# Last MLP of a four-layer network: its norm moved beside the products of the MLP in front of it, a second PSUM bank, its load and stores on another queue

## The chip, the core and the metric

The kernel runs on one core of a Trainium2 chip. The metric is the device time of one execution in microseconds. A core has engines that run side by side[...]: PE (matrix products into PSUM), DVE (VectorE), ACT (ScalarE), POOL (GpSimd) and SP, which here only issues transfers. Transfers are issued from SP, ACT and POOL and carried by 16 DMA engines. [...]a bank that a product was summed in has to be read out by ACT or DVE before the next product may use it.

## What is computed

The reference is a chain of four layers on x of shape 8 x 384 x 32 x 32, all in float32. Layers 0 and 1 are state-space ("Mamba") blocks over 1024 tokens per image; layer 1 ends in a norm and an MLP. Layers 2 and 3 are depthwise convolutions, with a 1x1 convolution between them. What bears on the change is the end of layer 1 and the start of layer 2:

```python
# layer 1, per image, tokens xs of width 384
mo = mo * (1.0 + mod[:, None, :])          # output products of the Mamba block, gated
xs = xs + mo
h = _ln(xs, n3_g, n3_b)
h = jax.nn.gelu(h @ fc1_w.T + fc1_b) @ fc2_w.T + fc2_b
xs = xs + h
# layer 2, on all 8 images
out = bn_eval(dwconv(x, w_lk, 1), ...)     # and six smaller depthwise kernels, summed
```

## The kernel before

Channels lie on the 128 partitions, so 384 channels are 3 blocks. Tokens are cut into halves of 512. A *unit* is one half image in one of the Mamba layers; there are 32, layer 0 and layer 1 interleaved. An *MLP* belongs to one half image of layer 1; there are 16. Each unit is a row of 48 items of its scan, and each item is a slot. All other work (norms, products, copies, loads, stores) is put into slots of this clock with `put(slot, function, ...)`, from a table `AT` of offsets; within a slot, entries marked `first` go ahead. The slots then fix the order of instructions on every engine; nothing is reordered later. When the units are over, the slots that are left are emitted in order: the output products of the last unit, the rest of the MLP in front of the last (first half of image 7) and the whole last MLP (second half of image 7).

The output products of a unit (`out_product`, line 599) are three blocks m of 6 products each in PSUM pool `mm` (two banks), with weights `wo`; each block also has a load of the residual (`residual`), on ACT a bias (`out_gate`), on DVE the sum (`out_add`) and on SP a store to `x2` (`out_store`). `AT['out']` gives the three blocks' slots: 0, 5 and 9.

An MLP has these steps. `norm` (line 726) issues the load of three blocks into tile `mx` (one buffer, so that it waits for the MLP in front), the mean (3 products), `centre` on DVE, three squares on ACT each followed by a variance product, then ACT's `rs_tables` and `rs_exp`, four operations `rs_newton` on POOL (line 396) and three `scale` on POOL (line 408). `mlp_up` (line 692) makes 12 products of 3 steps each with weights `wi` (five buffers); `mlp_raw` on ACT copies each out of its bank into `fh`; four batches of gelu on ACT work on three tiles each, with a table load before and after. `mlp_down` (line 705) makes 3 output blocks of 12 steps from `fh` and weights `wo` (six slices, three buffers). `mlp_out` on DVE adds bias and residual `mo` (one buffer) into the tile `rows_out` (one buffer), and `mlp_store` (line 719) sends it to `x3`, 16 rows of 38 floats in each partition. Products of all MLPs are summed in one bank, pool `m_f`:

```python
ps_f = st.enter_context(tc.tile_pool(name="m_f", bufs=1, space=PSUM))
```

All these loads and stores are on SP's queue, in the order of the slots.

The depthwise layers are a class of their own, `Depthwise`, whose instructions are emitted after all slots. On POOL it clears four image tiles `xp` (line 952), then `early` issues the weight windows `wt` of the first ten groups (line 959, four loads each), then three tiles `q_out` of the 1x1 convolution are cleared (line 1020), and then `images` (line 973) loads image rows from `x3`, two loads a group. A group is 8 channels, so 16 groups need only the first block of `x3`. Weights of later groups are loaded from SP and ACT, ten groups ahead. Per group DVE shifts copies (lines 988 to 990), PE makes 32 products (line 997), ACT copies them out and stores.

Of the kernel before, what the change touches and what calls it, by code (L numbers as in the profile page):

```python
# [9 lines left out]
F32 = mybir.dt.float32  # L10
AF = mybir.ActivationFunctionType
ALU = mybir.AluOpType
# [4 lines left out]
P = 128  # L17
B = 8
C = 384
# [6 lines left out]
T = 512  # L26
NU = B * L // T
# [39 lines left out]
class Plan:  # L67
# [6 lines left out]
    def put(self, slot, f, *args, first=False):  # L74
        self.slots.setdefault(slot, ([], []))[0 if first else 1].append(lambda: f(*args))
# [141 lines left out]

AT = {'in_ahead': 3, 'out_ahead': 2, 'taps_ahead': 4, 'norm': (-5, -2, -1, 0, 1, 2, 3, 3, 5, 5, 7, 7, 11, 12, 13), 'x': (14, 16, 18, 24, 26, 29), 'shift': 1, 'conv': 4, 'u': 5, 'silu': ((28, 3, 0), (34, 6, 0), (40, 6, 3), (57, 6, 6)), 'hid': 2, 'ranks': (33, 34, 35), 'z': (31, 34, 36, 38, 40, 41), 'B': (40, 43, 47, 48), 'C': (42, 45, 47, 52), 'repeat': (9, 12, 12, 13), 'out': (0, 5, 9), 'out_half': 3, 'out_add': 4, 'out_gate': 2, 'res_ahead': 1, 'heads': 15, 'softmax': (17, 18, 19), 'attend': (19, 22, 25, 26), 'context': 28, 'hidden': (29, 30, 32, 35, 36, 39), 'gates': (47, 41, 46), 'mlp': 22, 'mlp_norm': (-7, 0, 1, 2, 3, 4, 5, 5, 5, 6, 6, 10, 10, 12, 12), 'mlp_plan': ((3, 62, 12, (21, 31, 42, 69), -2), (2, 42, 6, (26, 30, 42, 46), -2), (2, 40, 4, (24, 26, 34, 40), -2), (2, 40, 3, (24, 26, 34, 36), -2), (2, 42, 7, (22, 28, 36, 36), -2)), 'fold0': (-145, -128), 'shifted': 1, 'bc_out': 37, 'store': 2, 'px_ahead': 2, 'pool': (0, 4), 'norm0': (-97, -89, -86, -85, -83, -80, -77, -75, -74, -73, -72, -71, -69, -69, -68), 'soft': ((37, 2), (45, 4), (62, 6)), 'du': 1, 'du_pace': 0, 'flat_u': 1, 'inject': 0, 'y': 25, 'fold': 0, 'var': 1, 'down_gap': 0, 'first': {'x': [2, 4, 7, 10, 13, 16], 'silu': [[14, 3, 0], [22, 6, 0], [34, 6, 2], [44, 6, 6]], 'ranks': [22, 24, 25], 'z': [29, 31, 31, 33, 34, 35], 'soft': [[29, 2], [33, 4], [60, 6]], 'bc_out': 29, 'B': [32, 34, 36, 39], 'repeat': [0, 0, 0, 1], 'C': [38, 43, 43, 46]}, 'fold0_step': (1, 7), 'norm1': (-3, -1, 0, 1, 2, 3, 4, 4, 8, 8, 10, 10, 12, 13, 13), 'prepare': (-40, 4),  # L220
}


def layers(tc, k, a, vec, x0, x1, x2, x3, lasting, got):
# [8 lines left out]
    nc = tc.nc  # L233
# [7 lines left out]
    with ExitStack() as st:  # L241
# [5 lines left out]
        ps_f = st.enter_context(tc.tile_pool(name="m_f", bufs=1, space=PSUM))  # L247
# [8 lines left out]
        t = tile("fh")  # L256
# [25 lines left out]
        rows_out = wp.tile([P, T // HW, WIDE], F32, name="rows_out")  # L282
# [15 lines left out]
        hid = wp.tile([P, KD], F32, name="hid")  # L298

        def mm():  # L300
            return ps_mm.tile([P, T], F32, tag="mm", name="mm")
# [62 lines left out]

        def load(s, src, tag):
            s.xt = work.tile([P, KC, T], F32, tag=tag, name=tag, bufs=1)
            nc.sync.dma_start(s.xt, src.rearrange("(c p) t -> p c t", p=P)[:, :, s.cols])

        def mean(s):
            s.mean = mm()  # L370
# [25 lines left out]
        def rs_newton(s, step):  # L396

            if step == 0:
                s.rt = work.tile([P, T], F32, tag="sq", name="sq", bufs=1)
                nc.gpsimd.tensor_tensor(s.rt, s.ry, s.ry, ALU.mult)  # L400
            elif step == 1:
                nc.gpsimd.tensor_tensor(s.rt, s.rt, s.rv, ALU.mult)
            elif step == 2:
                nc.gpsimd.tensor_scalar(s.rt, s.rt, -0.5, 1.5, ALU.mult, ALU.add)
            else:
                nc.gpsimd.tensor_tensor(s.ry, s.ry, s.rt, ALU.mult)

        def scale(s, c):
            nc.gpsimd.tensor_tensor(s.xt[:, c], s.xt[:, c], s.ry, ALU.mult)


        def product(s, m):
# [274 lines left out]
        class Mlp:  # L687
            def __init__(self, b, half):
                self.b, self.half, self.cols = b, half, slice(half * T, (half + 1) * T)
                self.w, self.ps, self.hs = {}, {}, [None] * KF  # L690

        def mlp_up(s, m, c):
            if c == 0:
                s.ps[m] = ps_f.tile([P, T], F32, tag="f", name="f")
            nc.tensor.matmul(s.ps[m], s.w["in", m][:, c], s.xt[:, c], start=c == 0, stop=c == KC - 1)  # L695

        def mlp_raw(s, m):
# [6 lines left out]

        def mlp_down(s, m, f):
            if f == 0:
                s.down = ps_f.tile([P, T], F32, tag="f", name="f")
            nc.tensor.matmul(  # L708
                s.down, s.w["out", 2 * m + f // KD][:, f % KD], s.hs[f], start=f == 0, stop=f == KF - 1
            )  # L710
# [7 lines left out]

        def mlp_store(s, m):
            n = T // HW  # L720
            nc.sync.dma_start(x3[m * P : (m + 1) * P, s.half * n : (s.half + 1) * n, s.b, :], rows_out)


        put = plan.put

        def norm(s, src, tag, at, slots):

            slots = iter([at + e for e in slots])
            put(next(slots), load, s, src, tag)
            put(next(slots), mean, s)  # L730
            put(next(slots), centre, s, first=True)
            for c in range(KC):
                e = next(slots)
                put(e, square, s, c)
                put(e + AT["var"], variance, s, c, first=AT["var"] > 0)
            put(next(slots), rs_tables, s, first=True)
            put(next(slots), rs_exp, s)
            for step in range(4):
                put(next(slots), rs_newton, s, step)
            for c in range(KC):  # L740
                put(next(slots), scale, s, c)
# [12 lines left out]
        for j, s in enumerate(folds):  # L754
            for m in range(2 * KD):
                at = (j - 1) * SLOTS + 7 + 2 * m if j else AT["fold0"][m // KD] + AT["fold0_step"][m // KD] * (m % KD)
# [9 lines left out]
        for b in range(1, B):  # L766
            order += [(1, b - 1), (0, b + 1)] if b < B - 1 else [(1, b - 1), (1, b)]
        units = [Unit(both[n], b, half) for n, b in order for half in range(L // T)]
        done = {(s.layer.gated, s.b, s.half): i for i, s in enumerate(units)}
        assert len(units) == 2 * NU  # L770

        for i, s in enumerate(units):

            lay, at = s.layer, (i - 1) * SLOTS
            first = AT if i else {**AT, **AT["first"]}
            norm(s, lay.src[s.b], "xt", at, AT["norm"] if i > 1 else AT[f"norm{i}"])
            for d in range(KD):
                e = at + first["x"][d]
# [44 lines left out]
            for d in range(KD):  # L823
                at = i * SLOTS + (d - 2) * PER
# [4 lines left out]
                put(at + AT["y"], y_out, s, d, first=True)  # L829

            at = (i + 1) * SLOTS
            for m in range(KC):
                e = at + AT["out"][m]
                put(e - AT["res_ahead"], residual, s, m)
                if lay.gated:
                    put(e + AT["out_gate"], out_gate, s, m)
                use_out(e, s, m, lay.w["out"][m])
                for j in range(2):
                    put(e + AT["out_half"] * j, out_product, s, m, j)
                put(e + AT["out_add"], out_add, s, m, first=True)  # L840
                put(e + AT["out_add"] + AT["store"], out_store, s, m, first=True)
            if not lay.gated:
                continue

# [28 lines left out]
        for b in range(B):  # L873
            for half in range(L // T):
                s = Mlp(b, half)
                at = max(at, (done[True, b, half] + 1) * SLOTS + AT["mlp"])
                if (at - AT["mlp"]) % SLOTS > 20:
                    at += (AT["mlp"] - at) % SLOTS
                pace_up, down, pace_down, tables, gap = AT["mlp_plan"][max(b - B + 4, 0) + (b == B - 1) * half]
                norm(s, x2[b], "mx", at, AT["mlp_norm"])  # L880
                for m in range(KF):
                    e = at + 12 + pace_up * m
                    use_in(e, s, m, fc1_w[m])
                    for c in range(KC):
                        put(e + c * pace_up // KC, mlp_up, s, m, c)
                    put(e + 2 * pace_up // KC + 1, mlp_raw, s, m, first=True)
                for j, e in enumerate(tables):
                    put(at + e, table, lambda s=s, j=j: s.hs[3 * j : 3 * j + 3], AF.Gelu_apprx_tanh)
                for m in range(KC):
                    e = at + down + (pace_down + AT["down_gap"]) * m  # L890
                    put(e, mlp_residual, s, m)
                    for f in range(KF):
                        if f % KD == 0:
                            use_out(e + f * pace_down // KF, s, 2 * m + f // KD, a["fc2"][2 * m + f // KD])
                        put(e + f * pace_down // KF, mlp_down, s, m, f)
                    put(e + pace_down, mlp_out, s, m, first=True)
                    put(e + pace_down + AT["store"], mlp_store, s, m, first=True)
                at += down + KC * (pace_down + AT["down_gap"]) + gap
# [316 lines left out]
```

## Time and profile before

| | us |
|---|---|
| median of 3 runs (lowest, highest) | 6904.85 (6898.36, 6907.45) |
| the profiled execution | 6903.45 |
| its span in the profile | 6901.6 |
| 6188.07 to 6229.88: last output products, end of the first products of the MLP in front | 41.8 |
| 6229.88 to 6266.6: output products of that MLP | 36.7 |
| 6266.6 to 6278.14: rest of the last MLP's norm | 11.5 |
| 6278.14 to 6330.34: its 12 first products | 52.2 |
| 6330.34 to 6366.83: its 3 output blocks | 36.5 |
| 6368.56 to 6552: first depthwise layer | 183.4 |
| 6552 to 6686: 1x1 convolution | 134 |
| 6686 to 6901.6: second depthwise layer | 215.6 |

The first part of the page gives the engines' busy time over the whole span:

```profile
PE 5854.2 (85%) x22562; PEld 2074.2 (30%) x22562; DVE 5757.2 (83%) x4591; ACT 4475.7 (65%) x7478; POOL 5276.5 (76%) x2830
```

These shares are those of the long scan stage, which fills the first nine tenths of the span. The change lies in about 180 us behind it, where the engines stand otherwise. There the bank of the MLPs is read out after every product, and PE waits 0.78 us for it each time (timeline of PE; start, duration, instruction, and in brackets the idle time before it with what ended it; a product of 128x512 appears as two records):

```profile
6288.03 2.84 PE L695 MATMUL f<-mx,wi 128*128 128x512 f32 x6 [0.78 <-ACT fh L699]
6291.65 2.84 PE L695 MATMUL f<-mx,wi 128*128 128x512 f32 x6 [0.78 <-ACT fh L699]
```

A line of the chain of waits gives start, duration, engine, tile and line; "issue" is time for which the profile shows no reason. A line of the stretches gives the length of the stretch, then busy time and count of instructions for PE, weight load, DVE, ACT and POOL, then PE's clock (1 is full), the DMA engines' busy share and GB/s.

### The profile page before, as it was taken

What the parts mean: (1) busy time and instruction counts of PE and PEld (TensorE: products, weight loads), DVE (VectorE), ACT (ScalarE), POOL (GpSimd) and SP (SyncE); (2) the same over time, 40 slices, a digit from 0 to 9 for tenths busy, and PEclk for the clock granted to TensorE, in tenths of its full rate; (3) what the DMA queues carried; (4) which work ended last, traced back from release to release, by engine and by line L of the source; (5) the groups of instructions that cost most, each with busy time, mean ns of one, the idle gap of its engine ahead of it and who ended that gap; (6) DMA issues with size and microseconds to landing.
All of it is one profiled execution on the core that took longest, in us unless ns stands there. A gap on an engine that the chain in (4) does not pass through costs nothing. (4 is left out here: it accounts for less than half of the span.)

```text
span 6901.6 us, 76776 instructions
## 1 busy us (share of the span) xinstructions
PE 5854.2 (85%) x22562; PEld 2074.2 (30%) x22562; DVE 5757.2 (83%) x4591; ACT 4475.7 (65%) x7478; POOL 5276.5 (76%) x2830
## 2 busy tenths in 40 slices
PE   6787787888888888889888888889898888978898
PEld 2222222222322232222222232223232222323645
DVE  2899999899889888889989888889888898881736
ACT  4777666767676766767676767777677667652222
POOL 2888888888888878888888888888878788763412
PEclk7889998999999999999999999999999989989999
DMA  4665565666666666666766665666676665755979
GB/s 124 166 173 156 152 162 154 166 172 166 177 161 172 160 168 163 166 161 173 168 166 171 166 179 156 170 170 167 161 167 168 157 171 158 173 114 127 277 215 228
DMA packets 948777, 1160.03 MB, mean 168 GB/s; under 512 B 304840, under 2 KB 541448, under 8 KB 948360
## 3 DMA queue, kind: packets, MB, share of 16 engines
q1 hardware_dynamic: 794568, 1064.73, 59.4%
q10 hardware_dynamic: 140736, 50.09, 3.0%
q0 software_dynamic: 13056, 40.29, 2.1%
q8 instruction: 183, 3.00, 0.2%
q14 instruction: 234, 1.92, 0.1%
HBM read 904.67 MB, written 199.49 MB: 160 GB/s over the span
## 5 line engine op out<-in xcount | busy, mean ns | idle before, releaser
L532 POOL TENSOR_TENSOR dbu<-B,ru 128x1024 f32<-128x1024 f32 x1536 | 3584.8, 2357 | 137.8 <-DMA B<-bc 64.1
L525 ACT ACTIVATE h<-rd,A 128x512 f32<-128x512 f32 x3072 | 2117.6, 691 | 863.8 <-DVE hc L561 524.0
L553 DVE TENSOR_TENSOR_SCAN h<-h,state,dbu 128x512 f32<-128x512 f32 x1152 | 1482.3, 1287 | 219.2 <-ACT h L525 80.2
L561 DVE TENSOR_TENSOR hc<-h,C 128x1024 f32<-128x1024 f32 x1152 | 1410.7, 1225 | 126.7 <-DMA C<-bc 15.1
L556 DVE TENSOR_TENSOR_SCAN h<-h,dbu 128x1024 f32<-128x1024 f32 x576 | 1318.0, 2288 | 237.0 <-ACT h L525 180.5
L572 POOL TENSOR_TENSOR hc<-dbu,C 128x1024 f32<-128x1024 f32 x384 | 903.3, 2352 | 728.6 <-DVE dbu L556 323.2
L583 PE MATMUL acc<-hc,fold 128*32 128x512 f32 x6144 | 1167.0, 665 | 336.1 <-DVE hc L561 253.8
L415 PE MATMUL mm<-xt,wi 128*128 128x512 f32 x2232 | 1111.5, 637 | 43.5 <-ACT delta L491 19.5
L695 PE MATMUL f<-mx,wi 128*128 128x512 f32 x1152 | 612.6, 640 | 138.3 <-ACT fh L699 107.0
L708 PE MATMUL f<-fh,wo 128*128 128x512 f32 x1152 | 586.4, 627 | 81.4 <-DMA wo<-in_fc_dram 66.1
L415 PEld LDWEIGHTS mm<-xt,wi 128*128 128x128 f32 x2232 | 419.4, 200 | 736.4 <-issue 438.1
L604 PE MATMUL mm<-u,wo 128*128 128x512 f32 x1152 | 573.2, 637 | 42.2 <-DMA wo<-in_l_out_dram 38.3
L583 PEld LDWEIGHTS acc<-hc,fold 128*32 128x32 f32 x6144 | 164.5, 112 | 1154.7 <-DVE hc L561 541.0
L553 DVE TENSOR_TENSOR_SCAN dbu<-h,state,dbu 128x512 f32<-128x512 f32 x384 | 470.4, 1267 | 9.9 <-ACT h L525 5.4
L556 DVE TENSOR_TENSOR_SCAN dbu<-h,dbu 128x1024 f32<-128x1024 f32 x192 | 437.8, 2280 | 37.5 <-ACT h L525 31.2
L439 PE MATMUL mm<-xp,taps 128*64 128x512 f32 x1536 | 411.1, 658 | 30.8 <-DMA xp<-xp 11.2
L973 POOL DMA_DIRECT2D xp<-x x192 | 127.2, 663 | 390.6 <-PE ps L997 179.6
L997 PE MATMUL ps<-xp,wt 128*32 128x256 f32 x6144 | 346.3, 383 | 44.6 <-ACT o L1002 31.0
L305 ACT ACT_TABLE_LOAD x289 | 370.8, 1283 | 5.9 <-PEq L1203 0.7
L580 PE MATMUL acc<-u,skip 128*128 128x512 f32 x384 | 229.1, 681 | 163.0 <-DVE u L588 162.7
L695 PEld LDWEIGHTS f<-mx,wi 128*128 128x128 f32 x1152 | 209.3, 196 | 498.2 <-issue 248.9
L425 ACT ACTIVATE xp<-mm,b_in 64x512 f32<-64x512 f32 x384 | 261.6, 681 | 139.0 <-PE mm L415 136.6
(151 smaller groups left out, 5694.5 us busy)
## 6 DMA issues: line engine op xcount, KB each, us to landing
ru<-uu SPq DMA_DIRECT2D x1536, 128.0 KB
rd<-dd SPq DMA_DIRECT2D x1536, 128.0 KB
wi<-w_in SPq DMA_DIRECT2D x372, 192.0 KB
xp<-xp SPq DMA_DIRECT2D x384, 128.5 KB
dd<-delta SPq DMA_DIRECT2D x192, 256.0 KB
uu<-delta SPq DMA_DIRECT2D x192, 256.0 KB
wo<-in_l_out_dram SPq DMA_DIRECT2D x96, 384.0 KB
wi<-fc_w SPq DMA_DIRECT2D x192, 192.0 KB
```

Of the source, the lines that this page charges most:

```text
L415: nc.tensor.matmul(s.ps[m], w[:, c], s.xt[:, c], start=c == 0, stop=c == KC - 1)
L439: nc.tensor.matmul(s.ps[d][64 * h : 64 * h + 64], taps[:, h, j], xp[h][:, 2 * j : 2 * j + T], start=j == 0, stop=j == 1,)
L525: nc.scalar.activation(y[:, q], s.dr[d][1][h][:, q], AF.Exp, scale=s.layer.A[:, at : at + 1])
L532: nc.gpsimd.tensor_tensor(dbu, s.B[g].unsqueeze(1).to_broadcast([P, 2, T]), s.ur[d][1][h], ALU.mult)
L553: nc.vector.tensor_tensor_scan(to[:, q], y[:, q], dbu[:, q], first, ALU.mult, ALU.add)
L556: nc.vector.tensor_tensor_scan(flat_to, flat_y, flat_b, first, ALU.mult, ALU.add)
L561: nc.vector.tensor_tensor(hc, to, s.C[g].unsqueeze(1).to_broadcast([P, 2, T]), ALU.mult)
L572: nc.gpsimd.tensor_tensor(hc, y, s.C[g].unsqueeze(1).to_broadcast([P, 2, T]), ALU.mult)
L583: nc.tensor.matmul(s.acc[d][32 * r : 32 * r + 32], k["fold"], tiles[r // 2][:, r % 2], start=False, stop=n == PER - 2)
L604: nc.tensor.matmul(s.ps[m], w[:, d], s.us[d], start=d == 0, stop=d == KD - 1)
L695: nc.tensor.matmul(s.ps[m], s.w["in", m][:, c], s.xt[:, c], start=c == 0, stop=c == KC - 1)
L708: nc.tensor.matmul(s.down, s.w["out", 2 * m + f // KD][:, f % KD], s.hs[f], start=f == 0, stop=f == KF - 1)
```

## The change

The line numbers of code behind line 690 move by 7 to 10. Seven things change, all in the last unit and the last MLP (`alone` is true for it only):

- The last unit's output blocks are put at slots 0, 2 and 4 in place of 0, 5 and 9, and the steps that belong to each block follow it more closely (`AT['last']`).
- The last MLP's norm gets its own offsets, `AT['alone']`. In PE's order its mean comes after 16 of the 36 output products of the MLP in front, its three variance products after 20, 24 and 28; before, the mean came after 32 and the variance products after all 36.
- Its newton and scale steps go to VectorE.
- Its products with odd number m are summed in a bank of pool `mm`, those with even m stay in the bank of `m_f`.
- The load of its `mx` is issued from POOL in place of SP.
- So are its three stores to `x3`.
- The lists in `AT['first']` become tuples, which changes nothing.

In POOL's order, the `mx` load and the three stores come where the seven norm operations were: behind POOL's last scan operation and ahead of the clearing of `xp`.

```diff
+ 'alone': (-9, -4, -3, -3, -2, -1, 1, 1, 1, 1, 1, 1, 1, 1, 1),
+ 'last': {'out': (0, 2, 4), 'res_ahead': 1, 'out_gate': 1, 'out_half': 1, 'out_add': 2, 'store': 1},
...
         def load(s, src, tag):
...
-            nc.sync.dma_start(s.xt, src.rearrange("(c p) t -> p c t", p=P)[:, :, s.cols])
+            s.queue.dma_start(s.xt, src.rearrange("(c p) t -> p c t", p=P)[:, :, s.cols])
...
-                nc.gpsimd.tensor_tensor(s.rt, s.ry, s.ry, ALU.mult)
+                s.side.tensor_tensor(s.rt, s.ry, s.ry, ALU.mult)
...
-            nc.gpsimd.tensor_tensor(s.xt[:, c], s.xt[:, c], s.ry, ALU.mult)
+            s.side.tensor_tensor(s.xt[:, c], s.xt[:, c], s.ry, ALU.mult)
...
+                self.alone = b == B - 1 and half == 1
+                self.side = nc.vector if self.alone else nc.gpsimd
+                self.queue = nc.gpsimd if self.alone else nc.sync
+
+            def bank(self, m):
+                return mm() if self.alone and m % 2 else ps_f.tile([P, T], F32, tag="f", name="f")
...
-                s.ps[m] = ps_f.tile([P, T], F32, tag="f", name="f")
+                s.ps[m] = s.bank(m)
...
-                s.down = ps_f.tile([P, T], F32, tag="f", name="f")
+                s.down = s.bank(m)
...
-            nc.sync.dma_start(x3[m * P : (m + 1) * P, s.half * n : (s.half + 1) * n, s.b, :], rows_out)
+            s.queue.dma_start(x3[m * P : (m + 1) * P, s.half * n : (s.half + 1) * n, s.b, :], rows_out)
...
+        for s in units:
+            s.side, s.queue = nc.gpsimd, nc.sync
...
+            out = {**AT, **AT["last"]} if i == 2 * NU - 1 else AT
             for m in range(KC):
-                e = at + AT["out"][m]
-                put(e - AT["res_ahead"], residual, s, m)
+                e = at + out["out"][m]
+                put(e - out["res_ahead"], residual, s, m)
...
-                norm(s, x2[b], "mx", at, AT["mlp_norm"])
+                norm(s, x2[b], "mx", at, AT["alone" if s.alone else "mlp_norm"])
```

More of the change, by code (lines that the diff above doesn't have):

```diff
@@ L216, in prepare @@
     yield
-AT = {'in_ahead': 3, 'out_ahead': 2, 'taps_ahead': 4, 'norm': (-5, -2, -1, 0, 1, 2, 3, 3, 5, 5, 7, 7, 11, 12, 13), 'x': (14, 16, 18, 24, 26, 29), 'shift': 1, 'conv': 4, 'u': 5, 'silu': ((28, 3, 0), (34, 6, 0), (40, 6, 3), (57, 6, 6)), 'hid': 2, 'ranks': (33, 34, 35), 'z': (31, 34, 36, 38, 40, 41), 'B': (40, 43, 47, 48), 'C': (42, 45, 47, 52), 'repeat': (9, 12, 12, 13), 'out': (0, 5, 9), 'out_half': 3, 'out_add': 4, 'out_gate': 2, 'res_ahead': 1, 'heads': 15, 'softmax': (17, 18, 19), 'attend': (19, 22, 25, 26), 'context': 28, 'hidden': (29, 30, 32, 35, 36, 39), 'gates': (47, 41, 46), 'mlp': 22, 'mlp_norm': (-7, 0, 1, 2, 3, 4, 5, 5, 5, 6, 6, 10, 10, 12, 12), 'mlp_plan': ((3, 62, 12, (21, 31, 42, 69), -2), (2, 42, 6, (26, 30, 42, 46), -2), (2, 40, 4, (24, 26, 34, 40), -2), (2, 40, 3, (24, 26, 34, 36), -2), (2, 42, 7, (22, 28, 36, 36), -2)), 'fold0': (-145, -128), 'shifted': 1, 'bc_out': 37, 'store': 2, 'px_ahead': 2, 'pool': (0, 4), 'norm0': (-97, -89, -86, -85, -83, -80, -77, -75, -74, -73, -72, -71, -69, -69, -68), 'soft': ((37, 2), (45, 4), (62, 6)), 'du': 1, 'du_pace': 0, 'flat_u': 1, 'inject': 0, 'y': 25, 'fold': 0, 'var': 1, 'down_gap': 0, 'first': {'x': [2, 4, 7, 10, 13, 16], 'silu': [[14, 3, 0], [22, 6, 0], [34, 6, 2], [44, 6, 6]], 'ranks': [22, 24, 25], 'z': [29, 31, 31, 33, 34, 35], 'soft': [[29, 2], [33, 4], [60, 6]], 'bc_out': 29, 'B': [32, 34, 36, 39], 'repeat': [0, 0, 0, 1], 'C': [38, 43, 43, 46]}, 'fold0_step': (1, 7), 'norm1': (-3, -1, 0, 1, 2, 3, 4, 4, 8, 8, 10, 10, 12, 13, 13), 'prepare': (-40, 4),
@@ new lines @@
+AT = {'in_ahead': 3, 'out_ahead': 2, 'taps_ahead': 4, 'norm': (-5, -2, -1, 0, 1, 2, 3, 3, 5, 5, 7, 7, 11, 12, 13), 'x': (14, 16, 18, 24, 26, 29), 'shift': 1, 'conv': 4, 'u': 5, 'silu': ((28, 3, 0), (34, 6, 0), (40, 6, 3), (57, 6, 6)), 'hid': 2, 'ranks': (33, 34, 35), 'z': (31, 34, 36, 38, 40, 41), 'B': (40, 43, 47, 48), 'C': (42, 45, 47, 52), 'repeat': (9, 12, 12, 13), 'out': (0, 5, 9), 'out_half': 3, 'out_add': 4, 'out_gate': 2, 'res_ahead': 1, 'heads': 15, 'softmax': (17, 18, 19), 'attend': (19, 22, 25, 26), 'context': 28, 'hidden': (29, 30, 32, 35, 36, 39), 'gates': (47, 41, 46), 'mlp': 22, 'mlp_norm': (-7, 0, 1, 2, 3, 4, 5, 5, 5, 6, 6, 10, 10, 12, 12), 'mlp_plan': ((3, 62, 12, (21, 31, 42, 69), -2), (2, 42, 6, (26, 30, 42, 46), -2), (2, 40, 4, (24, 26, 34, 40), -2), (2, 40, 3, (24, 26, 34, 36), -2), (2, 42, 7, (22, 28, 36, 36), -2)), 'fold0': (-145, -128), 'shifted': 1, 'bc_out': 37, 'store': 2, 'px_ahead': 2, 'pool': (0, 4), 'norm0': (-97, -89, -86, -85, -83, -80, -77, -75, -74, -73, -72, -71, -69, -69, -68), 'soft': ((37, 2), (45, 4), (62, 6)), 'du': 1, 'du_pace': 0, 'flat_u': 1, 'inject': 0, 'y': 25, 'fold': 0, 'var': 1, 'down_gap': 0, 'first': {'x': (2, 4, 7, 10, 13, 16), 'silu': ((14, 3, 0), (22, 6, 0), (34, 6, 2), (44, 6, 6)), 'ranks': (22, 24, 25), 'z': (29, 31, 31, 33, 34, 35), 'soft': ((29, 2), (33, 4), (60, 6)), 'bc_out': 29, 'B': (32, 34, 36, 39), 'repeat': (0, 0, 0, 1), 'C': (38, 43, 43, 46)}, 'fold0_step': (1, 7), 'norm1': (-3, -1, 0, 1, 2, 3, 4, 4, 8, 8, 10, 10, 12, 13, 13), 'alone': (-9, -4, -3, -3, -2, -1, 1, 1, 1, 1, 1, 1, 1, 1, 1), 'last': {'out': (0, 2, 4), 'res_ahead': 1, 'out_gate': 1, 'out_half': 1, 'out_add': 2, 'store': 1}, 'prepare': (-40, 4),
@@ L399, in rs_newton @@
                 s.rt = work.tile([P, T], F32, tag="sq", name="sq", bufs=1)
-                nc.gpsimd.tensor_tensor(s.rt, s.ry, s.ry, ALU.mult)
+                s.side.tensor_tensor(s.rt, s.ry, s.ry, ALU.mult)
             elif step == 1:
-                nc.gpsimd.tensor_tensor(s.rt, s.rt, s.rv, ALU.mult)
+                s.side.tensor_tensor(s.rt, s.rt, s.rv, ALU.mult)
             elif step == 2:
-                nc.gpsimd.tensor_scalar(s.rt, s.rt, -0.5, 1.5, ALU.mult, ALU.add)
+                s.side.tensor_scalar(s.rt, s.rt, -0.5, 1.5, ALU.mult, ALU.add)
             else:
-                nc.gpsimd.tensor_tensor(s.ry, s.ry, s.rt, ALU.mult)
+                s.side.tensor_tensor(s.ry, s.ry, s.rt, ALU.mult)
         def scale(s, c):
-            nc.gpsimd.tensor_tensor(s.xt[:, c], s.xt[:, c], s.ry, ALU.mult)
+            s.side.tensor_tensor(s.xt[:, c], s.xt[:, c], s.ry, ALU.mult)
         def product(s, m):
@@ L831, in layers @@
             at = (i + 1) * SLOTS
+            out = {**AT, **AT["last"]} if i == 2 * NU - 1 else AT
             for m in range(KC):
-                e = at + AT["out"][m]
-                put(e - AT["res_ahead"], residual, s, m)
+                e = at + out["out"][m]
+                put(e - out["res_ahead"], residual, s, m)
                 if lay.gated:
-                    put(e + AT["out_gate"], out_gate, s, m)
+                    put(e + out["out_gate"], out_gate, s, m)
                 use_out(e, s, m, lay.w["out"][m])
                 for j in range(2):
-                    put(e + AT["out_half"] * j, out_product, s, m, j)
-                put(e + AT["out_add"], out_add, s, m, first=True)
-                put(e + AT["out_add"] + AT["store"], out_store, s, m, first=True)
+                    put(e + out["out_half"] * j, out_product, s, m, j)
+                put(e + out["out_add"], out_add, s, m, first=True)
+                put(e + out["out_add"] + out["store"], out_store, s, m, first=True)
             if not lay.gated:
```

## The prediction

> **What bounds the kernel now.** I read the page first (shares, then the 40 slices), then the chain of waits from 6180 us to the end, then the timelines of PE, POOL and SP there, and last the busy time of the two stages of the depthwise layer. The change touches only the last unit's output products, the MLP behind them and the last MLP, so only the piece from 6188 us (last scan) to 6368.56 us (first depthwise product) can move by itself.
>
> ```profile
> span 6901.6 us, 76776 instructions
> POOL 2888888888888878888888888888878788763412
> DMA  4665565666666666666766665666676665755979
> ```
>
> Slice 37 of 40 (6211 to 6384 us) is the piece in question: POOL drops to 6 and below, so it has room. The chain there, times from the span's start:
>
> ```profile
> 6276.84 1.26 POOL mx L409
> 6278.10 0.04 issue
> 6278.14 5.50 PE f L695 x6
> 6283.65 0.02 issue
> 6283.67 0.70 ACT fh L699
> 6284.37 0.04 issue
> 6284.41 2.86 PE f L695 x6
> ...
> 6353.56 7.02 DMA wo<-in_fc_dram
> 6360.58 0.04 issue
> 6360.62 5.42 PE f L708 x12
> 6366.04 2.52 issue
> 6368.56 11.59 PE ps L997 x177
> ```
>
> The norm's last multiplication on POOL releases the first product of the last MLP; after each product the single bank `f` is emptied by ACT (0.78 us of PE idle each time); the last output product waits for a weight slice; and depthwise products follow 2.5 us later. They can do so because POOL has done their preparation beside the last MLP:
>
> ```profile
> 6280.47 8.64 POOL L952 MEMSET xp<- 128x2528 f32 x4
> 6289.06 6.52 POOL L959 DMA_DIRECT2D wt<-k_rows  x11
> ...
> 6315.56 0.58 POOL L959 DMA_DIRECT2D wt<-k_rows  x1 [1.58 <-DMA wt<-k_rows]
> 6316.13 3.19 POOL L1020 MEMSET q_out<- 128x1824 f32 x2
> 6329.63 1.62 POOL L1020 MEMSET q_out<- 128x1824 f32 x1 [10.30 <-PE f L695]
> 6350.45 4.36 POOL L973 DMA_DIRECT2D xp<-x  x8 [19.20 <-DMA x<-rows_out]
> ```
>
> Four memsets, 40 weight loads, three memsets, then the images, in that order, each behind the one before it. Afterwards DMA is full, and the stage takes 183.5 us for 48 groups:
>
> ```profile
> 6368.50:6422.00 53.50, 53.44 (x960) 45.21 (x964) 51.45 (x63) 12.80 (x27) 16.73 (x29) 0.97 1.05 272
> 6422.00:6552.00 130.00, 116.94 (x2120) 81.57 (x2111) 100.56 (x128) 32.68 (x69) 58.37 (x84) 0.99 1.03 276
> ```
>
> The first column is PE's busy time, the last three are clock, DMA share and GB/s: PE is full only for the first 15 groups, DMA throughout.
>
> **What the Trainium skill says.** "DMA: Bandwidth & Descriptors", in "Anatomy of one DMA", states that DMA engines do not wait on semaphores: a wait happens on the issuing sequencer before dispatch. The trace agrees: POOL stood 19.20 us before its image load, and the memset at 6316.13 came only after a load that had itself waited 1.58 us. "PSUM — Partial Sum Buffer", in "Engine vs sequencer instructions", calls the GpSimd queue strict FIFO; the timeline above shows nothing overtaking. "TensorE: Matmul & The Clock Gate", in Part 1, says that the clock halves after an idle window of some 3.4 us and needs as long to come back; here six records took 5.49 us after 7.78 us of idleness, against 2.84; but also 4.54 after 2.14 us, so this trace shows it at shorter waits than the page's window.
>
> **The change part by part.**
> *Output products closer (0, 2, 4).* The same 18 products of `mm` and 21 of `f` run after 6188.07. The weight slices of the next product are no longer behind a late store on SP, so the 2.19 us wait for `wo` goes. But the `f` products now end as a run of 13 in one bank, and ACT has a gelu batch (1.28 + 1.67 + 1.28 us) between the tenth and the eleventh copy. Step by step, product by product at 0.88 us and 0.78 us for each copy, the eleventh product ends at 6227.8, its copy at 6229.9: the `wo` products start at 6229.9, as before (6229.88). Worth nothing.
>
> *Norm inside those products.* 36 products at 0.88 us, one bank wait of 0.85, and now 3 mean and 3 variance products (0.87 each) between them: 6229.9 + 31.65 + 0.85 + 5.2 = 6267.6. The third variance product ends 8 products (7.0 us) before that; ACT needs 2.0 us (0.69, 0.58, 0.53 and gaps), and VectorE seven operations of 128x512. Their nearest rows are L588 at 0.69 and half of L561's 1.225 us, so 4.3 to 4.8 us instead of POOL's 7.9: ready by 6267.4, hidden. The load of `mx`, now from POOL, starts when the last `f` product frees the tile (6227.8) and has 17 us until the mean. What is late next is SP: the twelve `wi` loads stand behind the store of the third output block.
>
> ```profile
> 6266.63 0.37 SPq L721 DMA_DIRECT2D x<-rows_out  x1
> 6267.05 41.71 SPq L310 DMA_DIRECT2D wi<-fc_w  x12
> ```
>
> Before, POOL hid this. Now the store goes at 6268.4 (0.8 us for the VectorE addition). The traffic after 6267.5 was 131 to 169 GB/s for 2.5 us and had moved store and first slice (0.31 + 0.20 MB) 3.9 us after the store's issue, all five slices after 6.9. I take 4.9: the first product at 6273.3, against 6278.14. The bounds are 4.1 and 7.4.
>
> *Two banks.* 12 x 2.64 us (a quarter of the 10.57 for 24 records) and 2.65 for the cold clock, 34.3 us. ACT's gelu batches are absorbed by the second bank but for 0.6 us at the tenth product: 34.9 instead of 52.20, so 6308.2. The output products need 3 x 10.55 us; their bank waits (2 x 0.84) go, and the `wo` wait of 2.04 shrinks to 0.8, since the image loads that shared the DMA are not there yet (bounds 0 and 1.8). They end at 6340.7, the last addition at 6341.5, against 6366.83: 25.3 us won.
>
> *Load and stores from POOL.* This is what decides. POOL's compiled order is now: `mx` load, the three stores, four memsets, 40 weight loads, three memsets, images. Each store waits for its VectorE addition, the third until 6341.5, and the whole preparation is queued behind it. SP is freed of its three stores, but nothing on SP was late except the weight slice already counted. After 6341.5: issue of the third store, which the trace doesn't show from POOL. A weight load of 256 runs takes 0.582 and an image load of 128 runs 0.550 us to issue; the slope gives 1.0 us for the store's 2048 runs of 152 bytes, nothing reasonable is below 0.6, and 6 us would be 3 ns for each run. I take 1.5. Then 8.64 (memsets), 40 x 0.587 = 23.5 for the issues plus some waiting (27.07 before, beside `wi` loads): 24.5. Then 4.86 for the memsets of `q_out`. Sum 39.5: the first image load is issued at 6381.0. It lands after 3.2, and two copies of 0.82 precede the first product.
>
> ```profile
> wt<-k_rows POOLq DMA_DIRECT2D x40, 128.0 KB, 4.7
> xp<-x POOLq DMA_DIRECT2D x4, 152.0 KB, 3.2
> ```
>
> So depthwise starts at 6385.9 instead of 6368.56, 17.3 us later. Once it runs, it needs the same transfers. Before, 6.4 us of other traffic (a store, the 576 KB of `pw`, weights of the eleventh group) stood in front when the first tiles were given back 3.5 us after its start; now that is done earlier, but DMA then idles until tiles come back. I count 1.3 us as won; the bounds are 0 and 6.4. The layers behind it are unchanged.
>
> **Sum.** +17.3 - 1.3 = +16.0 on the profiled execution's own 6903.45 us (1.85 around its span): 6919.5. That execution is 1.4 us below the median of the runs shown, 6904.85, so it is +0.21% against the median.
>
> **Rivals.**
> 1. Depthwise takes up more. For: DMA share 1.03 to 1.05, and the early traffic is out of its way. If all 6.4 us come back, and the weight loads are issued without a wait (-1), 6903.45 + 17.3 - 6.4 - 1.0 = 6913.4, no change that can be told. Against: loads for later groups are asked for only when PE frees a tile, so an empty DMA earlier doesn't help.
> 2. POOL pays more for the stores. For: 2048 short runs each on the page's "software_dynamic" queue, eight times the runs of any load seen from POOL. Six us per store (+4.5), the weight loads at 27 (+2.5) and `wi` at the late bound (+2.5) give 6929. Against: the small slope between 128 and 256 runs.
> 3. The other side: POOL's waiting stores don't hold up what is behind them. Then the 39.5 us lie beside the last MLP as before, depthwise starts 2 to 3 us after 6341.5, and the time is about 6903.45 - 24.5 = 6879. It turns faster once more than 17 of the 39.5 us are hidden. For: only that no wait of POOL for VectorE with a store stands in this trace. Against: the 19.20 and 1.58 us waits, both held up what followed.
> That the change misses its aim (norm and banks give nothing) is not likely: the 0.78 us waits have one cause each.
>
> **Numbers.** Forecast 60%, rival 1 16%, rival 2 20%, rival 3 4%. What a measurement here can tell from no change is about 0.2%, 13.8 us, so the line is at 6918.7, and the forecast's own spread of about 5 us lies across it: two thirds of it, 40%, above. Slower 40 + 20 = 60%, within 20 + 16 = 36%, faster 4%. Range: downwards rival 1 with the earlier `wi` and no `wo` wait (-1.6) gives about 6911; upwards rival 2 with a second cold clock (+1.7) and 1 us more at `wo` 6932.
>
> **What would show it.** The last MLP's `f` and `mm` products without ACT between them, 35 us in all; its last addition near 6341; then POOL: store, 8.6 us of memsets, 40 loads in about 24 us, memsets, and the chain running through POOL L969 and L1030 with PE idle some 45 us; the first depthwise product near 6386; the stage after it about 182 us long. It is wrong if the POOL memsets lie before the last addition (rival 3), if a POOL store is several us long (rival 2), or if depthwise takes under 179 us (rival 1).

## The result and the profile after

The changed kernel took 6919.28 us (median of 20 runs, 6912.04 to 6931.80), the kernel before, run beside it, 6904.56 us (20 runs, 6890.48 to 6920.64). The ratio is 1.002 with a 95% interval of 1.0013 to 1.0028: slower by 0.2%, some 15 us. The forecast was 6919.5 us. The profiled execution of after took 6926.64 us; its page shows, in the lines of span, POOL and DMA over 40 slices:

```profile
span 6924.9 us, 76767 instructions
POOL 2888888888788878888888878887878788662413
DMA  4665555666656666666666665666666666744979
```

Slice 37 (6232 to 6405 us) is the piece in question: POOL has 2 and DMA 4, where before they had 3 and 5 (the "6" that the prediction names is slice 36). The slices don't hold quite the same work, since slice 37 of before has 15.4 us of the depthwise layer in it and that of after 4.4. Taken from the last unit's first output product to the first depthwise product, POOL was busy 48.8 of 180.5 us before and 45.4 of 196.5 us after, and the DMA share fell from 0.44 to 0.38. So both do less in the time in which the end is set; the 9 of slice 38, the depthwise layer, is as it was.

The spans differ by 23.3 us, more than the medians. Where the difference lies is read at four instructions that both programs have:

| us | before | after | difference |
|---|---|---|---|
| start to the last unit's first output product (L604) | 6188.07 | 6204.65 | +16.6 |
| from there to the first depthwise product | 180.49 | 196.45 | +16.0 |
| to the first product of the 1x1 convolution | 190.54 | 188.68 | -1.9 |
| to the first product of the second depthwise layer | 136.73 | 136.50 | -0.2 |
| to the end | 205.77 | 198.62 | -7.2 |

The first row and the last two contain the same instructions in both kernels. In the ten profiles of this study the first row goes from 6188.07 to 6209.10 us, and not with the change: it is scatter from one execution to the next, with chips mixed in. The last row, between 198.6 and 205.8 us in the ten, scatters too. The second row is what the change touches; below it is called the stretch, and its length is compared.

The chain of waits of after, in the stretch (start, duration, what the end waited for):

```profile
6285.32 5.18 DMA wi<-fc_w
6290.63 5.46 PE f L702 x6
6296.09 2.98 PE mm L702 x6
...
6352.48 5.43 PE f L715 x12
6357.93 0.76 DVE rows_out L721
...
6360.12 8.66 POOL xp L962 x4
6368.78 5.61 POOL wt L969 x10
...
6394.87 1.57 POOL q_out L1030
6396.44 2.88 DMA xp<-x
6399.40 0.79 DVE xp L998
6400.22 0.79 DVE xp L999
```

Before, the chain went from the last output product straight to the depthwise product. Now it goes through POOL: memsets, weight loads, memsets and only then an image. The timeline of POOL over the same time (start, busy time, instruction and count, idle time before it and what ended it) shows why they stand there:

```profile
6242.88 0.96 POOL L367 DMA_DIRECT2D mx<-x  x1 [45.99 <-PE f L702]
6337.09 1.19 POOL L728 DMA_DIRECT2D x<-rows_out  x1 [93.25 <-DVE rows_out L721]
6347.67 1.15 POOL L728 DMA_DIRECT2D x<-rows_out  x1 [9.39 <-DVE rows_out L721]
6358.98 1.15 POOL L728 DMA_DIRECT2D x<-rows_out  x1 [10.15 <-DVE rows_out L721]
6360.12 8.66 POOL L962 MEMSET xp<- 128x2528 f32 x4
6368.71 23.05 POOL L969 DMA_DIRECT2D wt<-k_rows  x40
6391.76 4.75 POOL L1030 MEMSET q_out<- 128x1824 f32 x3
6396.44 5.51 POOL L983 DMA_DIRECT2D xp<-x  x8
```

POOL stands still for 93.25, 9.39 and 10.15 us in front of three stores, each of which waits for an addition. The preparation of the depthwise layer, which needs none of these sums, starts after the third. On PE the same thing is one line, 43.21 us of idleness:

```profile
6401.10 19.22 PE L1007 MATMUL ps<-xp,wt 128*32 128x256 f32 x308 [43.21 <-DMA xp<-x]
```

The gain that the change has ahead of this is real: from L604 to the end of the last addition it is 154.0 us (6204.65 to 6358.68), against 178.8 before. It won 24.7 us there and gave back 40.7 between the addition and the first depthwise product (42.4 us instead of 1.7).

### The profile page after: what moved, and what is told of

Its sections match the earlier page's. It is cut to its first block, busy times and chain, and to the rows that moved or that the text cites. A ratio compares the mean times of both kernels' runs of the same rounds, so it can differ in the third digit from the quotient of the medians.

```text
span 6924.9 us, 76767 instructions
## 1 busy us (share of the span) xinstructions
PE 5875.9 (85%) x22562; PEld 2080.5 (30%) x22562; DVE 5759.1 (83%) x4598; ACT 4475.9 (65%) x7478; POOL 5287.3 (76%) x2827
## 4 chain that ended last, share of the span: by engine, by line
PE 15%; DVE 10%; DMA 9%; ACT 7%; issue 4%; POOL 3%; SPq 1%; ACTq 1%; DVEq 0%; POOLq 0%
DVE h L553 3%; DVE h L556 3%; PE mm L415 3%; ACT h L525 2%; PE f L715 2%; DMA rd<-dd 2%; PE ps L1041 2%; DMA wt<-k_rows 2%; POOL dbu L532 2%; PE acc L583 1%; PE f L702 1%; DVE hc L561 1%; DVE dbu L556 1%; PE mm L604 1%; ACT L305 1%
## 5 line engine op out<-in xcount | busy, mean ns | idle before, releaser
L702 PE MATMUL f<-mx,wi 128*128 128x512 f32 x1116 | 589.2, 635 | 128.5 <-ACT fh L706 101.1
L604 PE MATMUL mm<-u,wo 128*128 128x512 f32 x1152 | 574.0, 638 | 40.7 <-DMA wo<-in_l_out_dram 39.9
L604 PEld LDWEIGHTS mm<-u,wo 128*128 128x128 f32 x1152 | 225.3, 204 | 401.2 <-issue 342.1
```

The lines of the kernel that those rows point to most:

```text
L604: nc.tensor.matmul(s.ps[m], w[:, d], s.us[d], start=d == 0, stop=d == KD - 1)
```

## The experiments

Theory A is the prediction's: the stores on POOL hold up what is queued behind them, and the rest of the change is a gain. Rivals for each run stand in its expectation. The runs below were made on three chips; the kernel before ran beside them on each, and its median there was 6905.29 us (the first four runs), 6902.76 (the next three) and 6924.16 (the last). So ratios are compared, and the stretch.

| run | median | ratio to before (95%) | stretch |
|---|---|---|---|
| before | | 1 | 180.5 |
| after | 6919.28 | 1.0020 (1.0013 to 1.0028) | 196.5 |
| after, stores on SP | 6885.25 | 0.9964 (0.9953 to 0.9976) | 160.5 |
| before, stores on POOL | 6944.27 | 1.0047 (1.0032 to 1.0061) | 217.5 |
| after, one store on POOL | 6910.88 | 1.0002 (0.9993 to 1.0012) | 184.1 |
| stores on SP, one bank | 6901.10 | 0.9992 (0.9984 to 1.0001) | 176.9 |
| stores on SP, slices ahead | 6878.23 | 0.9961 (0.9949 to 0.9973) | 155.2 |
| the same, norm on POOL | 6877.13 | 0.9964 (0.9952 to 0.9975) | 151.0 |
| the same, outputs as before | 6882.41 | 0.9962 (0.9948 to 0.9976) | 152.4 |
| the same, stores on ACT | 6895.36 | 0.9957 (0.9943 to 0.9971) | 153.2 |

### The stores back on SP

```diff
 # after, mlp_store
-            s.queue.dma_start(x3[m * P : (m + 1) * P, ...], rows_out)
+            nc.sync.dma_start(x3[m * P : (m + 1) * P, ...], rows_out)
```

> The changed kernel with only the three stores of the last MLP back on SP; the mx load stays on POOL. Theory (POOL's preparation waits behind the third store): the preparation lies beside the MLPs again, the first depthwise product follows the last addition by about 2 to 3 us in place of 42, the stage behind it is some 2 us longer as before the change: 6919.3 - 39.4 + 1.9 = about 6882 us, from the last scan's end to the first depthwise product about 157 us against 196 (changed) and 180 (before). Rival A (the 5.2 MB of early weights collide with the wo slices when they are loaded this early): the MLP in front of the last takes 5 to 10 us more, 6887 to 6892. Rival B (POOL is not what holds the depthwise layer): 6910 or more.

Measured: 6885.25 us, ratio 0.9964, and a stretch of 160.5 us instead of 196.5. One line of code turns the change from slower than before to faster. The wait of 43.21 us is gone; instead there is another, in the timelines of PE and of POOL:

```profile
6287.49 5.01 PE L702 MATMUL f<-mx,wi 128*128 128x512 f32 x6 [11.03 <-DMA wi<-fc_w]
6349.53 7.11 PE L715 MATMUL f<-fh,wo 128*128 128x512 f32 x12 [2.03 <-DMA wo<-in_fc_dram]
6359.17 6.19 PE L1007 MATMUL ps<-xp,wt 128*32 128x256 f32 x77 [2.52 <-issue]
```

```profile
6237.90 8.65 POOL L962 MEMSET xp<- 128x2528 f32 x4
6246.49 6.93 POOL L969 DMA_DIRECT2D wt<-k_rows  x12
6276.58 5.17 POOL L969 DMA_DIRECT2D wt<-k_rows  x9 [23.17 <-PE f L715]
```

The first depthwise product follows the last addition by 1.7 us, as before. But the first product of the last MLP now waits 11.03 us for its weight slice, against 6.54 in after. POOL is free, so it starts the depthwise weights early. After twelve loads it is held until the last output product of the MLP in front is done, and the other 28 go out from 6276.58, just as SP issues the slices (6277.69). The first slice is used 9.8 us after its issue, in after 5.3. The time lies between the expected 6882 and the rival's 6887 to 6892. The rival had named the collision, but at the weights of the outputs and not at those of the first products, where most of it is. The stage behind was expected to be 2 us longer than in after; it was not (188.2 against 188.7).

### Only the stores on POOL

```diff
 # before, mlp_store
-            nc.sync.dma_start(x3[m * P : (m + 1) * P, ...], rows_out)
+            (nc.gpsimd if s.b == B - 1 and s.half == 1 else nc.sync).dma_start(x3[m * P : (m + 1) * P, ...], rows_out)
```

> The kernel before with nothing changed but the three stores of the last MLP, moved to POOL. Theory: store 1.15, memsets 8.66, weight loads 23.05, memsets 4.75, first image 3.0 and two copies 1.7 come after the last addition (6366.8 in the profile of before), so depthwise starts 42 us after it in place of 1.7; less about 2 us in the stage behind and 1.3 at the wait for wo: 6904.6 + 40.5 - 3.3 = about 6942 us. Rival: POOL's preparation is hidden or costs little; then 6905.

Measured: 6944.27 us, ratio 1.0047; the stretch is 217.5 us, 37.0 longer than before. After minus the run above is 36.0. The median had been expected at about 6942. The stores on POOL cost the same with and without the rest of the change. Seen closer, the first depthwise product follows the last addition 40.9 us later than in before, and in after 40.7 later than in the run above; what remains are waits for weights and slow clocks ahead of the addition. The timeline of POOL is that of after, 19 us later:

```profile
6377.83 1.15 POOL L721 DMA_DIRECT2D x<-rows_out  x1 [10.23 <-DVE rows_out L714]
6378.97 8.65 POOL L952 MEMSET xp<- 128x2528 f32 x4
6387.56 21.25 POOL L959 DMA_DIRECT2D wt<-k_rows  x37
```

### Only the first store on POOL

```diff
 # after, mlp_store
-            s.queue.dma_start(x3[m * P : (m + 1) * P, ...], rows_out)
+            (s.queue if m == 0 else nc.sync).dma_start(x3[m * P : (m + 1) * P, ...], rows_out)
```

> The changed kernel with only the first of the three stores on POOL, the second and third on SP. Theory (dose): POOL is let go by the first addition, 21.9 us earlier than by the third in the changed kernel's profile, so the first depthwise product comes 21.9 us earlier: 6919.3 - 21.9 = about 6897 us. Rival (the cost is in issuing three stores from POOL, 1.15 us each, or in the DMA, not in the place of the third): within 3 us of 6919.

Measured: 6910.88 us, stretch 184.1: 12.3 us less than after, where the distance between the first and the third addition says about 22. The direction is right and the size is not. The reason is seen on POOL, whose weight loads now have to wait for transfers:

```profile
6336.52 1.20 POOL L728 DMA_DIRECT2D x<-rows_out  x1 [93.42 <-DVE rows_out L721]
6337.71 8.65 POOL L962 MEMSET xp<- 128x2528 f32 x4
...
6355.77 4.60 POOL L969 DMA_DIRECT2D wt<-k_rows  x8 [1.70 <-DMA wt<-k_rows]
...
6371.50 0.58 POOL L969 DMA_DIRECT2D wt<-k_rows  x1 [2.25 <-DMA wt<-k_rows]
```

They take from 6346.29 to 6378.70, 32.4 us instead of the 23.05 of after, as they now run beside what SP issues in that time: a `wo` slice, two stores, `pw` and the weights of the eleventh group. That is 9.4 of the 9.6 us missing. Beside the last MLP each load is dearer, but what is still hidden is more than what it adds.

### One bank

```diff
 # the kernel with its stores on SP, Unit.bank
-                return mm() if self.alone and m % 2 else ps_f.tile([P, T], F32, tag="f", name="f")
+                return ps_f.tile([P, T], F32, tag="f", name="f")
```

> Stores on SP as in the run of that name, and the last MLP again in one PSUM bank. Theory: the 12 first products take 52.2 us in place of 34.9 (the bank is read out after each, and the clock drops in the waits), and two bank waits of 0.84 come back in the output products: about 18 us more than with two banks, 6882 + 18 = about 6900 us. Rival (the early weights are what the last MLP then hides, or ACT is the bound): less than 8 us more.

Measured: 6901.10 us, 16 us more than with two banks, near the 18 expected and twice the rival's 8; the stretch is 16.4 us longer. PE's timeline has the old form again:

```profile
6310.28 2.84 PE L702 MATMUL f<-mx,wi 128*128 128x512 f32 x6 [0.78 <-ACT fh L706]
6315.26 4.48 PE L702 MATMUL f<-mx,wi 128*128 128x512 f32 x6 [2.14 <-ACT fh L706]
```

Two banks are worth 16 us, which is most of the 20.0 us by which the stretch with the stores on SP is shorter than before. Of the norm's new place little is left there, as its 11.5 us of before are replaced by 11.03 us of waiting for `wi`.

### The slices ahead of the stores

```diff
 # the kernel with its stores on SP, first products of the MLPs
-                    use_in(e, s, m, fc1_w[m])
+                    put(e - (14 if s.alone else AT["in_ahead"]), slice_in, s, m, fc1_w[m])
```

On SP two `wi` slices of the last MLP then stand in front of the last two stores of the MLP in front of it, and a third between these two stores. (The expectation has all three in front of both.)

> The kernel after with the stores of the last MLP back on SP's queue, and the first three weight slices of its products put ahead of the last two stores of the MLP in front, so that they don't stand behind stores that wait for additions. My theory: in the run with the stores on SP alone, TensorE waited 11.03 us for the first slice, and the first six records then took 5.01 us instead of 2.74, a cold clock; the slices were issued only at 6277.7, when the last store had got its sum. With three ahead that wait goes, and the fourth, issued at about 6277.6 and needed some 8 us later, is 2 to 3 us late: about 10 us won. From the last scan's output product to the first depthwise product about 151 us (160.5 before), the median about 6876 us. Rival: the slices are late because the depthwise weights that POOL loads in the same microseconds fill the DMA engines, so the order on SP changes little: over 158 us, and a median above 6882 us.

Measured: 6878.23 us, ratio 0.9961, and 155.2 us of stretch, 5.3 less than the run with the stores on SP. In the profile the 11.03 us are gone; the fourth slice, behind the last store, is late as expected (2.06 us):

```profile
6269.32 2.84 PE L702 MATMUL f<-mx,wi 128*128 128x512 f32 x6 [0.84 <-DVE rows_out L721]
...
6279.37 2.84 PE L702 MATMUL mm<-mx,wi 128*128 128x512 f32 x6 [2.06 <-DMA wi<-fc_w]
...
6333.32 8.39 PE L715 MATMUL f<-fh,wo 128*128 128x512 f32 x12 [3.77 <-DMA wo<-in_fc_dram]
```

From the end of the output products in front to the end of the twelve first products it takes 35.1 us instead of 45.1: a gain of 10.0 us, of which 8.1 are less waiting and most of the rest the slow clock of the first records. Part of it goes back at the last `wo` slice, 3.0 us more than in the run with the stores on SP (1.74 of wait, 1.28 of slow clock), and 1.7 in a slow clock at the first output block of the MLP in front (12.26 us for 24 records, against 10.57). The stretch lies between the expected 151 and the rival's 158: for the first slice the rival, DMA traffic alone, is out, and what went back was not in my sum. By the ratios, 0.9961 and 0.9964, the two kernels can't be told apart; the gain is shown in the profiles only.

### The norm on POOL again

```diff
 # the kernel with slices ahead, Unit
-                self.side = nc.vector if self.alone else nc.gpsimd
+                self.side = nc.gpsimd
```

> The kernel with stores on SP and three slices ahead, with the last MLP's norm on POOL again instead of VectorE, at the same place in the order of work. My theory: what the change wins with the norm is its place beside the products of the MLP in front, not the engine. POOL takes some 8.2 us for what VectorE does in 4.55, so its first scaled chunk is about 2 us later, at about the end of the products in front, and the memsets and weight loads behind it on POOL have over 50 us until the depthwise needs them: the same to 3 us slower than with VectorE (6876 to 6879 us if that one is 6876). Rival: the engine carries the gain, as POOL's norm ends on the path and its weight loads follow it late: 6 us or more slower.

Measured: 6877.13 us, ratio 0.9964, no difference to 0.9961; the stretch is 151.0, not longer but 4.2 us shorter. The timelines of PE and POOL:

```profile
6280.67 3.57 PE L702 MATMUL f<-mx,wi 128*128 128x512 f32 x6 [0.93 <-POOL mx L409]
6284.07 2.74 PE L702 MATMUL mm<-mx,wi 128*128 128x512 f32 x6
```

```profile
6274.84 1.03 POOL L400 TENSOR_TENSOR sq<-rs_y 128x512 f32<-128x512 f32 x1 [33.68 <-ACT rs_y L394]
...
6279.35 3.71 POOL L409 TENSOR_TENSOR mx<-mx,rs_y 128x512 f32<-128x512 f32 x3
6282.99 8.64 POOL L962 MEMSET xp<- 128x2528 f32 x4
```

POOL's norm ends later, but PE waits only 0.93 us for its first block. The weight loads behind it start at 6291.58, 11 us after the first slice is used, and the fourth slice is no longer waited for. So at its new place the norm is hidden on either engine, where before PE waited 7.78 us for it; VectorE has no value that these runs show. No run put the norm back to its old place alone, so what the place is worth by itself is read from these waits.

### The output products as before

```diff
 # the kernel with slices ahead
-            out = {**AT, **AT["last"]} if i == 2 * NU - 1 else AT
+            out = AT
```

> The kernel with stores on SP and three slices ahead, with the last unit's output products at the distances of the kernel before. My prediction gave this part of the change nothing; the two profiles showed 40.06 us instead of 41.81 from the last scan's output product to the first product of the MLP in front, 1.75 us. My theory: 0 to 2 us slower than with the closer products. Rival: the closer products bring the norm's input forward and carry the overlap: 4 us or more slower.

Measured: 6882.41 us, 4.2 more than the run with slices ahead, but the ratio, 0.9962, is the same within its interval, and the stretch is 152.4 us, not longer. The 1.75 us of the expectation (41.81 against 40.06 us up to the first output product of the MLP in front) came from a slow clock. These are the first L604 lines of the timeline of PE, of before and then of after:

```profile
6188.07 4.54 PE L604 MATMUL mm<-u,wo 128*128 128x512 f32 x6
```

```profile
6204.65 2.84 PE L604 MATMUL mm<-u,wo 128*128 128x512 f32 x6
```

Six records took 1.70 us more in before. This run has the 4.54 too, and 41.86 us; the run of before with its stores on POOL has 2.84 and 40.3 us with the old distances. The closer output products are worth nothing, as predicted.

### The stores on ScalarE's queue

```diff
 # the kernel with slices ahead, mlp_store
-            nc.sync.dma_start(x3[m * P : (m + 1) * P, ...], rows_out)
+            (nc.scalar if s.alone else nc.sync).dma_start(x3[m * P : (m + 1) * P, ...], rows_out)
```

> The kernel with three slices ahead, with the last MLP's three stores on ScalarE's queue instead of SP's. Behind them ScalarE has only the first depthwise activation, which waits for the depthwise's products anyway. My theory: with the stores on SP the last weight slice of the outputs is late (3.77 us of wait and 8.39 us instead of 5.3 for the last twelve records, a cold clock) because it stands behind a store of short runs on SP's own queue; with the stores on another queue the wait is under 1 us, as it was with the stores on POOL (0.74 us), and POOL stays free: some 4 to 6 us won, about 150 us from the last scan's output product to the first depthwise product (155.2 with the stores on SP), the median about 6873 us. It also says again that what costs is the place on POOL and not the stores leaving SP. Rival: the slice is late because the store's short runs fill the same DMA engines whichever queue they come from: a wait of 3 us or more stays, 154 us or more.

Measured: ratio 0.9957, stretch 153.2 us; on this chip the kernel before took 6924.16, so the median of 6895.36 is compared with that. The stores leave SP, POOL stays free, and depthwise follows the last addition at once: what costs 36 us is the place in POOL's queue, not that the stores leave SP. The theory on `wo` falls, however: the stretch lies nearer the rival's 154 than the expected 150. The wait at the last slice is 2.76 us, and there is one of 1.72 at the slice before:

```profile
6341.02 5.42 PE L715 MATMUL mm<-fh,wo 128*128 128x512 f32 x12 [1.72 <-DMA wo<-in_fc_dram]
...
6354.35 5.42 PE L715 MATMUL f<-fh,wo 128*128 128x512 f32 x12 [2.76 <-DMA wo<-in_fc_dram]
```

The slice is used 6.7 us after its issue, in slices ahead 7.7, in after 4.7. So the queue in front of the slice is not the whole of it. In after two other things differ as well. POOL's image loads share the DMA here (and in slices ahead at 6323.02, 2.6 us ahead of the slice's issue); in after they come 49 us later than the slice:

```profile
6342.92 4.37 POOL L983 DMA_DIRECT2D xp<-x  x8 [17.39 <-DMA x<-rows_out]
```

And the store from POOL started late: in the trace's DMA packets the slice of after was through at 6352.04 and the store's first packet came at 6352.35, while here the store's packets begin at 6350.11 and run beside the slice's (6350.93 to 6353.89). In all ten profiles the slice is used within 4.9 us of its issue where POOL loads nothing beside it (after, only the stores on POOL) and after 5.9 to 7.7 us where POOL loads images or weights (the other eight). That fits the prediction's reason, that images not yet loaded leave room for `wo`. But in those eight a store from SP or ACT runs there too, and no run separates the images from the store.

## Why the prediction was right

Step by step, as it put them, in the profiled execution of after:

| step | predicted | measured |
|---|---|---|
| output products closer | 0 | 0 (1.70 of the difference is a slow clock) |
| norm hidden beside the products in front, on VectorE | 4.3 to 4.8 us, hidden | 4.54 us (6279.13 to 6283.67), ready 0.4 before they end |
| wait for `wi` after the end of those products | 5.7 | 6.54 |
| 12 products with two banks | 34.9 | 34.90 |
| wait for `wo` | 0.8 | 0.74 |
| won up to the last addition | 25.3 | 24.7 |
| third store, issue on POOL | 1.5 | 1.15 |
| memsets | 8.64 | 8.66 |
| 40 weight loads | 24.5 | 23.05 |
| memsets of `q_out` | 4.86 | 4.75 |
| addition to first depthwise product | 44.4 | 42.4 |
| later start of depthwise | 17.3 | 16.0 |
| depthwise stage | -1.3 | -1.9 |

The mechanism is the one predicted, and it is shown from both sides: taking the stores off POOL removes 36.0 us, putting them there alone adds 37.0, and with them on another queue than SP or POOL the cost is absent too. Rival 3, that the waiting stores don't hold up what follows, is refuted by the 93.25, 9.39 and 10.15 us in POOL's timeline. Its number, 6879 us, came near to what the kernel does without that wait (6885). Rival 2 is refuted: a store of 2048 runs took 1.15 to 1.19 us to issue, and the slope from two small loads gave 1.0. Its ground, that POOL's queue has eight times the runs of a load to move, doesn't show in the packets either: the trace has 80 for such a store and 32 for a weight load. Rival 1's 179 us was not reached: the prediction counted the stage to 6552 us (183.4), the tables here to the first 1x1 product (190.5), and 1.9 less is 181.5 by its count.

Two small terms were off. The wait for `wi` was 0.8 longer, within its bounds. The weight loads were 1.4 shorter, because POOL never had to wait between them; at 0.576 us each they lie 0.5 below even the 23.5 that the prediction gave for issuing alone. The end of the products in front came 79.4 us after L604 where the sum has 79.5, but by luck: 1.75 us less ahead of the first output product, and 1.7 more in it (12.26 us for 24 records, against 10.57), nearly all of it the clock. The term for the stage, -1.3, has about the size measured, but its reason is not shown. It was that other traffic would be out of the way, and the first 53.5 us do have a DMA share of 0.93 instead of 1.05 (stretches of after; the last three columns are clock, DMA share and GB/s):

```profile
6401.10:6454.60 53.50, 53.49 (x948) 39.19 (x952) 50.27 (x63) 12.36 (x26) 18.98 (x31) 0.95 0.93 253
```

Yet the run with stores on SP, where depthwise starts at once, has a stage of 188.2 us, as short as after's 188.7, and the run of before with its stores on POOL, where it starts late, has 190.0. Those two contradict the reason. The stage takes 185.8 to 188.7 us in all eight profiles with the changed MLP and 190.0 and 190.5 in the two with the old one, so a shorter stage goes with the rest of the change and not with the late start; why is open.

The forecast's 16.0 us against 14.7 between the medians is also a fortunate match: the two profiled executions lie 23 us apart, and only because rows with the same instructions were set aside can the 16.0 of the stretch be seen.

## What to carry to other kernels

A transfer that waits for a result held everything behind it on its issuing engine, here on POOL and, at the `wi` slices, on SP. Before moving one to a less busy queue, list what that queue has to do next and whether it needs the result. The busy share of the engine doesn't tell: POOL had 3 tenths in this slice before, and nearly all that it did there was due at the end of it. And when a stage is shortened or an engine made free, look at which loads then start earlier and what they meet: here the wait for `wi` grew by 4.5 us when the queue was clear and the depthwise weights came early.

## What the runs showed of the hardware

A store of 2048 runs of 152 bytes took 1.15 to 1.36 us to issue from POOL, against 0.58 for a weight load of 256 runs: eight times the runs, twice the time. Counted in the DMA packets of the traces it is less strange: the store is 2048 packets of 152 bytes from SP (before, 6367.80 to 6369.84), but 80 of 4104 and 3040 bytes from POOL (after, 6360.78 to 6362.86), and a weight load from POOL is 32 of 4096.

The clock of PE drops after short waits, and not always after the same one. In front of the first output block of the MLP in front PE waited 2.14 us in seven of the profiles; the 24 records behind took 12.26 us in three of them (after, one store on POOL, slices ahead) and 10.57 in four (stores on SP, one bank, norm on POOL, stores on ACT). What goes with it in all seven is where the wait falls. In each of the ten traces the granted clock changes only at times that are multiples of 3.413 us apart (318 to 354 changes, none more than 0.003 us off). In the three slow cases the 2.14 us lie whole in one such interval, and the next runs at half clock; in the four others a boundary cuts them, and no interval has more than 1.55. The stretches around the wait in after and then in the run with the stores on SP (PE's busy time is the second figure, its clock the third from the end):

```profile
6242.16:6245.57 3.41, 1.27 (x3) 0.49 (x3) 0.00 (x0) 3.36 (x4) 0.96 (x1) 1.00 0.17 40
6245.57:6248.98 3.41, 3.41 (x5) 1.35 (x4) 0.00 (x0) 3.34 (x5) 0.00 (x0) 0.50 0.47 191
...
6237.29:6240.70 3.41, 1.93 (x5) 0.97 (x6) 0.00 (x0) 3.37 (x5) 3.41 (x3) 1.00 0.43 159
6240.70:6244.12 3.42, 3.42 (x10) 1.51 (x9) 0.00 (x0) 2.28 (x3) 3.42 (x2) 1.00 0.19 74
```

Over the ten traces (but for their first 50 us), all 1042 full-clock intervals with 2.1 us or more of idle PE were followed by one at half clock, and 116 of the 13738 with less than 1 us; between the two both occur. "TensorE: Matmul & The Clock Gate" of the Trainium skill, in Part 1, has an idle window of some 3.4 us: the length of the interval agrees, but it need not be idle throughout. A slow clock is worth 1.7 us each time here, as much as several steps of the sum, and it comes and goes between runs with the same waits, so a difference of this size in a single profile need not be the change's.
